# A decoder layer on one core: moments of two norms as ScalarE passes, and the feed-forward product behind the third block

## The chip, the cores and the metric

The kernel runs on one core of a Trainium2 chip. A core has five engines, each with its own queue of instructions that it works through in order: TensorE (PE in the profile, with its weight loads as PEld), VectorE (DVE), ScalarE (ACT), GpSimd (POOL) and SyncE (SP, which here issues the DMAs). They meet only at semaphores: an instruction that needs another engine's result waits, and everything behind it on its engine waits with it. The metric is the device time in microseconds, median of several runs.

## The reference

Three sublayers, each followed by a layer norm: causal attention, a long convolution, and a linear layer, the first and last with ternary weights and 8-bit activations. Cut to what the change touches:

```python
def _layernorm(x, axis=-1, eps=1e-05):
    m = jnp.mean(x, axis=axis, keepdims=True)
    v = jnp.var(x, axis=axis, keepdims=True)
    return (x - m) / jnp.sqrt(v + eps)

# convolution: x is (16 batches, 256 rows, 512), 32 heads of 8 rows, causal along the 512
kv = jnp.einsum('bhil,bhjl->bijhl', k_, v_)
y = irfft(rfft(kv, n=1024) * rfft(ssm_kernel, n=1024), n=1024)[..., :512]
out = jnp.einsum('bijhl,bhil->bjhl', y + kv * D, q_)

# linear layer on each row of 512
rms = rsqrt(mean(x * x) + 1e-06)
xn = x * rms * gamma
a_scale = 127.0 / (max(abs(xn)) + 1e-05)
x_q = clip(round(xn * a_scale), -128.0, 127.0) / a_scale
ffn = x_q @ w_q.T          # w_q ternary

x = _layernorm(x + attention(x))
x = _layernorm(x + convolution(ctx, ctx, x))
x = _layernorm(x + ffn(x))
```

The two norms of this case are the second and the third. The second norm's moments also give the root mean square that the linear layer divides by.

## The kernel before, in words

The attention comes first and takes about half of the time; the change doesn't touch it. It leaves the normed activations in `x1t`, turned so that the 512 positions lie along the partitions.

The second stage treats the 32 heads of the convolution one after another, with one repetition of a Python loop per head. A head has 8 rows in 16 batches, so its result is a tile of 128 x 512. The convolution is done as matrix products with a Toeplitz matrix of taps, `w`, cut into four blocks of 128 positions. Because it is causal, output block `lb` needs the input blocks 0 to `lb`: blocks 0, 1, 2 and 3 need 1, 2, 3 and 4 of them. Each is two products of 288 columns in float32, which the trace records as two matmuls each; so the four blocks show as x4, x8, x12 and x16 on L785.

For each head the engines do this:

- **GpSimd** multiplies the context with itself shifted (`multiply`, L754) into `kv`, and ScalarE squares it (`square`, L760). After each block GpSimd sums the parts (`add`, L960 and L962).
- **TensorE** makes the block's product `y` (`products`, L785) and turns the summed parts back into rows of 512 (`read`, L820), which gives `tok`. `y` has two accumulators, so a block takes the one that the block two before it has left: block 1 of a head can't start before VectorE has read block 3 of the head before.
- **VectorE** multiplies `y` with the queries in five instructions per block (`with_queries`, L797 to L812).
- **The second norm** of the previous head, `tok`, is made in the same repetition. `second_moments` takes mean and variance; `engine_roots` (L845, ScalarE), `newton` (L851 VectorE, L855 ScalarE) and `inverse_roots` (L863) make inverse roots out of a quarter of each variance; `second_centred` (L878) makes the centred, weighted row `xn`, `second_max` (L882) its largest size, and `second_norm` the normed row `x2` (L888), the scale, and the integers `fi` (L899 and L188).
- **The linear layer**: `turn` has the integers transposed by a DMA into `fit` (L904, on SP's queue); `feed_forward` multiplies them with the weights (L909), adds `x2` (L911, which gives `r3`) and takes the moments of `r3`; `finish` makes the third norm (L926) and sends it out (L927).

Both sets of moments come from VectorE: `bn_stats` (L835), `bn_aggr` (L837) and, for each root that is needed, the scaled variance `quarter` (L840). The square roots of `r3` of one head and of `tok` of the next are taken together, in one call with three columns.

The order on every engine is written out by hand: the stage runs inside `manual_schedule`, and each engine gets its instructions in the order in which the Python code issues them. So the place of a call in the loop sets its place in the queue of every engine that it uses. `on(stage, h, ...)` calls a stage for head `h` where there is such a head. In repetition `h` the blocks of head `h` are made, the second norm of head `h - 1`, and the linear layer and third norm of head `h - 2`. `last_heads` ends the work for the last two heads.

Of the kernel before, what the change touches and what calls it, by code (L numbers as in the profile page):

```python
# [9 lines left out]
F32 = mybir.dt.float32  # L10
# [5 lines left out]
P = 128  # L16
# [16 lines left out]
def decoder_kernel(ctx: ExitStack, tc: tile.TileContext, x, ctx_t, w_q, w_k, w_v, w_o, ker, d_skip, gamma, w_f, out):  # L33
# [695 lines left out]
    with ExitStack() as l2:  # L729
# [2 lines left out]
        ps_y = l2.enter_context(tc.tile_pool(name="ps_y", bufs=2, space=PSUM, side="right"))  # L732
        pb = l2.enter_context(tc.tile_pool(name="pb", bufs=1, side="right"))
        gam = pb.tile([P, E], F32, name="gam")
        op = l2.enter_context(tc.tile_pool(name="op", bufs=4, side="right"))


# [93 lines left out]
        FORMS = ((1.0, LN_EPS), (1.0, LN_EPS), (1.0 + RMS_EPS, RMS_EPS * LN_EPS))  # L831

        def moments2(src, roots, forms):
            st = sm.tile([P, 6], F32, name="st2")
            nc.vector.bn_stats(st, src)  # L835
            mv = sm.tile([P, 2], F32, name="mv2")
            nc.vector.bn_aggr(mv, st)  # L837
            for i in forms:
                a, b = FORMS[i]
                nc.vector.tensor_scalar(roots.quarter[:, i : i + 1], mv[:, 1:2], a / 4, b / 4, ALU.mult, ALU.add)  # L840
            return mv[:, 0:1]

        def engine_roots(roots):
            c = roots.cols
# [19 lines left out]

        def shifted(mean, res):
            shift = sm.tile([P, 1], F32, name="shift")
            nc.vector.tensor_scalar(shift, mean, res, -1.0, ALU.mult, ALU.mult)
            return shift

        def second_moments(m, roots):  # L870


            m.flat = m.tok.rearrange("p c k -> p (c k)")
            m.mean = moments2(m.flat, roots, (1, 2))

        def second_centred(m):
            m.xn = fp.tile([P, E], F32, name="xn")
            nc.vector.scalar_tensor_tensor(m.xn, m.flat, m.mean, gam, ALU.subtract, ALU.mult)  # L878

        def second_max(m):  # L880
            m.amax = sm.tile([P, 1], F32, name="amax2")
            nc.vector.tensor_reduce(m.amax, m.xn, AX.X, ALU.max, apply_absolute_value=True)  # L882

        def second_norm(m, roots, early_max=False):
            rstd, both = (roots.res[:, i : i + 1] for i in (1, 2))
            shift = shifted(m.mean, rstd)
            m.x2 = fp.tile([P, E], F32, name="x2")
            nc.scalar.activation(m.x2, m.flat, AF.Identity, bias=shift, scale=rstd)  # L888
            if not early_max:
                second_max(m)  # L890
            amax = m.amax
            nc.vector.tensor_scalar(amax, amax, both, 1e-5, ALU.mult, ALU.add)
            mul = sm.tile([P, 1], F32, name="mul2")
            nc.vector.reciprocal(mul, amax)
            nc.vector.tensor_scalar(mul, mul, both, 127.0, ALU.mult, ALU.mult)
            m.inv = sm.tile([P, 1], F32, name="inv2")
            nc.vector.tensor_scalar(m.inv, amax, w_inv[:, 4:5], 1.0 / 127.0, ALU.mult, ALU.mult)
            m.ft = fp.tile([P, E], F32, name="fq_t", tag="q_t")
            nc.scalar.activation(m.ft, m.xn, AF.Copy, bias=MAGIC, scale=mul)  # L899
            m.fi = rounded(fp, "fq", m.ft)  # L900

        def turn(m):
            m.fit = fp.tile([P, NB, P], BF16, name="fit")
            nc.sync.dma_start_transpose(m.fit, m.fi)  # L904

        def feed_forward(m, roots):
            acc = ps2.tile([P, E], F32, name="acc_f", tag="misc")
            for c in range(NB):
                nc.tensor.matmul(acc, m.fit[:, c, :], wf[:, c, :], start=(c == 0), stop=(c == NB - 1))  # L909
            m.r3 = fp.tile([P, E], F32, name="r3")  # L910
            nc.vector.scalar_tensor_tensor(m.r3, acc, m.inv, m.x2, ALU.mult, ALU.add)  # L911
            m.mean3 = moments2(m.r3, roots, (0,))

        def finish(m, roots, h, shared=False):
# [65 lines left out]
        def roots_of(cols):  # L980
            roots = Roots()
            roots.quarter = sm.tile([P, 3], F32, name="quarter")
            roots.root = sm.tile([P, 3], F32, name="root")
            roots.cols = cols
            return roots

        def last_heads():

            prev, last = heads[XH - 2 :]
            two, one, end = roots_of(slice(1, 3)), roots_of(slice(0, 1)), roots_of(slice(0, 1))  # L990
            read(last, 2)
            read_all(last, 3)
            second_moments(last, two)
            engine_roots(two)
            second_centred(last)
            newton(two)
            second_max(last)
            inverse_roots(two)
            second_norm(last, two, early_max=True)
            feed_forward(prev, one)  # L1000
            last.fit = fp.tile([P, NB, P], BF16, name="fit")
            transposed(ps2, last.fit, last.fi)
            engine_roots(one)
            newton(one)
            inverse_roots(one)
            finish(prev, one, XH - 2)
            feed_forward(last, end)
            engine_roots(end)
            newton(end)
            inverse_roots(end)  # L1010
            finish(last, end, XH - 1, shared=True)
# [5 lines left out]
        with tc.manual_schedule(engines=by_hand):  # L1017
            load(first_head, 0)
            load(heads[1], 1)
            nc.sync.dma_start(gam, gamma.partition_broadcast(P))  # L1020
            multiply(first_head, 1)
            multiply(first_head, 2)
            acc = {0: turn_sums(m, 0)}
            divide_sums(m)
            acc[1] = turn_sums(m, 1)
            keep(k, B - 3, (1,))
            m.ots, m.last = {}, {}
            for t in range(NT):
                divide(m, t, acc[t])
                out_scales(m, slice(t, t + 1))  # L1030
                m.ots[t] = scaled(ap, f"oq{t}", m.o[:, t, :], m.mul_o[t])
                if t == 0:
                    moments(n)
            multiply(first_head, 3)
            square(first_head)
            m.oit = kp.tile([P, NT, NB, P], BF16, name="oit")
            transposed(ps, m.oit[:, 0], rounded(ap, "oq0", m.ots[0]))
            close(m, slice(0, 1))
            transposed(ps, m.oit[:, 1], rounded(ap, "oq1", m.ots[1]))
            normalize(n)  # L1040
            moments_one(m, 0)
            keep(n, B - 2, (0,))
            multiplied(first_head, 0)
            normalize_one(m, 0)
            keep(m, B - 1, (0,))
            copy(first_head, slice(0, 1))
            copy(first_head, slice(1, NB))
            block(first_head, 0)
            close(m, slice(1, 2))
            moments_one(m, 1)  # L1050
            multiplied(first_head, 1)
            block(first_head, 1)
            normalize_one(m, 1)
            keep(n, B - 2, (1,))
            multiplied(first_head, 2)
            keep(m, B - 1, (1,))
            l1.close()
            fp = l2.enter_context(tc.tile_pool(name="fp", bufs=2))
            sm = l2.enter_context(tc.tile_pool(name="sm", bufs=3))
            ps_k = l2.enter_context(tc.tile_pool(name="ps_k", bufs=2, space=PSUM))  # L1060
            ps2 = l2.enter_context(tc.tile_pool(name="ps2", bufs=2, space=PSUM))


            for h in range(XH):
                roots = roots_of(slice(0 if h > 1 else 1, 3))

                on(load, h + 2, h + 2)
                on(add, h - 1, 3)
                on(block, h, 0)
                on(read, h - 1, 2)  # L1070
                on(multiply, h + 1, 1)
                on(square, h + 1)

                on(block, h, 1)
                on(feed_forward, h - 2, roots)
                on(add, h, 0)
                on(read, h - 1, 3)
                on(multiply, h + 1, 2)
                on(second_moments, h - 1, roots)
                if h > 0:  # L1080
                    engine_roots(roots)
                on(second_centred, h - 1)
                if h > 0:
                    newton(roots)

                on(block, h, 2)
                on(copy, h + 1)
                if h > 0:
                    inverse_roots(roots)
                on(add, h, 1)  # L1090
                on(read, h, 0)
                on(finish, h - 2, roots, h - 2)
                on(multiply, h + 1, 3)
                on(second_norm, h - 1, roots)

                on(block, h, 3)
                on(add, h, 2)
                on(read, h, 1)
                on(turn, h - 1)
            last_heads()  # L1100


# [35 lines left out]
```

## Time and profile before

| | us |
|---|---|
| median of 3 runs | 863.49 (861.42 to 866.24) |
| profiled execution | 861.06 |
| its span, first to last instruction | 859.2 |

The profiled execution lasts 1.9 us longer than its span. Its busy time by stage, in us:

| stage | length | PE | PEld | DVE | ACT | POOL | granted clock of TensorE |
|---|---|---|---|---|---|---|---|
| attention, 0 to 439.8 | 439.8 | 400.88 | 270.64 | 339.25 | 251.57 | 219.72 | 1.00 |
| handover, to 460.3 | 20.5 | 18.08 | 13.06 | 7.90 | 9.05 | 10.11 | 0.83 |
| head loop, to 842.9 | 382.6 | 371.84 | 271.48 | 335.67 | 159.39 | 352.67 | 1.00 |
| end, to 859.2 | 16.3 | 3.71 | 1.34 | 8.48 | 5.96 | 0.00 | 0.70 |

Times on the timeline count from the start of the span. A line gives start and length, engine, line of the code, operation, what it writes and reads, and in brackets how long the engine had been idle before it and what released it. Lengths of neighbours on one engine can overlap a little. In a line of waits the three numbers are the total, how many, and the longest.

### The profile page before, as it was taken

The page shows a single profiled execution, that of the slowest core. Times are in us where ns is not written, and L with a number is a line of the kernel's source. Part 1 is how long each engine was busy: PE and PEld are TensorE (multiplying, and loading weights), DVE is VectorE, ACT ScalarE, POOL GpSimd, SP SyncE. Part 2 cuts the span into 40 slices and gives each one's busy share as a digit, 9 for nine tenths or more (in the row PEclk, how much of TensorE's full clock was granted, in tenths as well). Part 3 has the DMA queues.
Part 4 walks back from the last instruction along what each step waited for, and adds up shares of the span by engine and source line. Part 5 has one row for each costly group of instructions (what it writes and reads, how often), then busy time and mean ns, then how long its engine had stood idle before and what let it go on. Part 6 is the DMA issues. An engine that isn't in the chain of part 4 may idle for free.

```text
span 859.2 us, 20181 instructions
## 1 busy us (share of the span) xinstructions
PE 794.5 (92%) x7677; PEld 556.5 (65%) x7754; DVE 691.3 (80%) x1889; ACT 426.0 (50%) x707; POOL 582.5 (68%) x652
## 2 busy tenths in 40 slices
PE   4889999999999999998878999999999999999993
PEld 3556666666666666665546777776777677777772
DVE  6757887788888778876665888988898888889886
ACT  6555655556565555655654334434443444344334
POOL 5265544545454454544638999999999999999980
PEclk9999999999999999999989999999999999999997
DMA  9121222233122222211320332333233323333311
GB/s 318 45 54 33 66 69 69 76 76 73 29 63 67 71 75 76 51 39 30 91 66 13 87 98 69 91 87 96 70 91 88 95 72 80 99 87 75 85 37 43
DMA packets 102207, 64.51 MB, mean 75 GB/s; under 512 B 66464, under 2 KB 83104, under 8 KB 102112
## 3 DMA queue, kind: packets, MB, share of 16 engines
q1 hardware_dynamic: 102112, 63.23, 27.5%
q8 instruction: 61, 1.00, 0.5%
q14 instruction: 34, 0.28, 0.1%
HBM read 43.34 MB, written 8.47 MB: 60 GB/s over the span
## 4 chain that ended last, share of the span: by engine, by line
PE 67%; DVE 12%; POOL 8%; ACT 6%; issue 6%; DMA 1%; ACTq 0%; DVEq 0%; POOLq 0%
PE y L785 23%; PE s L341 6%; PE acc L293 6%; PE s L381 5%; ACT p L386 4%; PE pv L409 4%; PE s L334 4%; DVE nmax L346 3%; PE acc_o L482 3%; POOL own L960 3%; PE acc_f L909 3%; POOL kv L754 3%; PE tok L820 3%; PE sums L416 2%; PE s L374 2%
## 5 line engine op out<-in xcount | busy, mean ns | idle before, releaser
L785 PE MATMUL y<-kv,w 128*128 128x288 f32 x1280 | 336.5, 410 | 3.7 <-DVE turn L812 2.7
L785 PEld LDWEIGHTS y<-kv,w 128*128 128x128 f32 x1280 | 234.7, 191 | 64.6 <-PE tok L820 8.5
L960 POOL TENSOR_TENSOR own<-own,turn 128x512 f32<-128x512 f32 x127 | 161.5, 1272 | 23.2 <-DVE turn L812 12.0
L390 POOL TENSOR_SCALAR_AFFINE_SELECT p<-p 128x512 f32<-128x512 f32 x128 | 81.0, 657 | 139.8 <-ACT p L386 129.5
L754 POOL TENSOR_TENSOR kv<-c 128x512 f32<-128x512 f32 (+1 forms) x128 | 144.0, 1136 | 2.9 <-PE sums L416 2.9
L346 DVE TENSOR_REDUCE nmax<-s 128x4 f32<-128x512 f32 (+1 forms) x128 | 116.5, 952 | 35.5 <-PE s L341 35.5
L386 ACT ACTIVATE p<-s 128x1536 f32<-128x1536 f32 x64 | 92.9, 1452 | 70.3 <-PE s L381 70.2
L845 ACT ACTIVATE root<-quarter 128x3 f32<-128x3 f32 (+2 forms) x34 | 6.9, 204 | 203.1 <-DVE quarter L840 203.0
L396 POOL TENSOR_TENSOR both<-p 128x512 f32<-128x512 f32 x64 | 82.3, 1285 | 5.3
L797 DVE SCALAR_TENSOR_TENSOR own<-y,q 128x128 f32<-128x128 f32 x128 | 36.0, 282 | 48.7 <-PE y L785 41.2
L962 POOL TENSOR_TENSOR own<-own 128x256 f32<-128x256 f32 x95 | 69.1, 727 | 7.5
L293 PE MATMUL acc<-xit,w 128*128 128x256 bf16 x504 | 68.9, 276 | 3.4 <-DVE w L158 3.2
L800 DVE TENSOR_TENSOR own<-y,q 128x384 f32<-128x384 f32 x128 | 70.0, 547 | 0.1
L803 DVE TENSOR_TENSOR turn<-y,q 128x384 f32<-128x384 f32 x128 | 70.0, 547 | 0.0
L293 PEld LDWEIGHTS <-w 128*128 128x128 bf16 x512 | 46.0, 99 | 24.0 <-issue 8.5
L820 PEld LDWEIGHTS tok<-ident,own 128*128 128x128 f32 x318 | 40.1, 141 | 32.7 <-POOL own L962 15.5
L820 PE MATMUL tok<-ident,own 128*128 128x128 f32 x318 | 57.2, 278 | 3.6 <-issue 1.2
L341 PE MATMUL s<-kt,qt 32*128 32x128 f32 (+1 forms) x1024 | 60.0, 348 | 0.0
L381 PE MATMUL s<-qt,kt 32*128 32x256 f32 (+1 forms) x1024 | 57.4, 335 | 0.0
L409 PE MATMUL pv<-p,va 128*32 128x256 f32 (+1 forms) x1024 | 54.9, 332 | 0.0
L421 ACT COPY ot<-pv 128x256 f32<-128x256 f32 x64 | 23.8, 373 | 50.9 <-PE pv L409 50.2
L334 PE MATMUL s<-mask,ident_h 128*128 128x256 bf16 x256 | 38.3, 271 | 11.1 <-ACT p L386 9.9
(148 smaller groups left out, 1342.0 us busy)
## 6 DMA issues: line engine op xcount, KB each, us to landing
xt<-in_x SPq DMA_DIRECT2D x16, 512.0 KB, 4.3
xr<-in_x SPq DMA_DIRECT2D x16, 512.0 KB, 4.7
c<-in_ctx_t SPq DMA_DIRECT2D x32, 256.0 KB, 3.3
w<-taps SPq DMA_DIRECT2D x32, 256.0 KB, 4.0
out_y<-res SPq DMA_DIRECT2D x31, 256.0 KB, 2.0
c<-in_ctx_t SPq DMA_DIRECT2D x32, 128.0 KB, 3.2
x1t<-in_w_q SPq DMA_DIRECT2D x1, 1024.0 KB, 6.4
x1t<-in_w_k SPq DMA_DIRECT2D x1, 1024.0 KB, 9.3
```

The source lines that it names most:

```text
L293: nc.tensor.matmul(acc[:, j, :], w[:, c, o * P : (o + 1) * P], m.xit[:, c].rearrange("p t k -> p (t k)"), start=(c == 0), stop=(c == NB - 1),)
L341: nc.tensor.matmul(s[:, r, lo:hi], m.qt[rows, g, q0 : q0 + P], m.kt[rows, g, 0:nk], start=False, stop=True, skip_group_check=True,)
L346: nc.vector.tensor_reduce(m.nmax[:, t, :, g], s[:, :, cols], AX.X, ALU.max, negate=True)
L381: nc.tensor.matmul(s[:, r, lo:hi], m.kt[rows, g, k0 : k0 + P], m.qt[rows, g, q0:S], start=False, stop=True, skip_group_check=True,)
L386: nc.scalar.activation(p, s[:, :, 0 : 3 * P], AF.Exp)
L390: nc.gpsimd.affine_select(out=own, in_=own, compare_op=ALU.is_ge, fill=0.0, base=0, pattern=[[0, 4], [1, P]], channel_multiplier=-1,)
L396: nc.gpsimd.tensor_tensor(both, p[:, :, P : 2 * P], p[:, :, 2 * P : 3 * P], ALU.add)
L409: nc.tensor.matmul(acc[rows, q0:S], m.va[:, j, 4 * g + r, :], p[:, r, src], start=(j == 0), stop=(j == 1), skip_group_check=True, tile_pos ...
L754: nc.gpsimd.tensor_tensor(kv[:, :, at : at + n * B].rearrange("p c (i b) -> p c i b", b=B), c[:, :, i : i + n, :], c[:, :, i + d : i + d + ...
L785: nc.tensor.matmul(y[:, Y0 + k * HALF : Y0 + (k + 1) * HALF], lhs, kv[:, mb, k * HALF : (k + 1) * HALF], start=(mb == 0), stop=(mb == lb),)
L820: nc.tensor.matmul(tok[:, lb, :], lhsT=own[:, d, :], rhs=ident, is_transpose=True, start=(d == last), stop=(d == 0))
L960: nc.gpsimd.tensor_tensor(own[:, 0:4, :], own[:, 0:4, :], turns[lb], ALU.add)
```

## The change

It does three things. The moments of both norms are no longer made by `bn_stats` and `bn_aggr` on VectorE, but by three ScalarE operations each: a copying pass whose accumulator gives the sum of the row, a step on one column that makes minus the mean, and a squaring pass with that as bias, whose accumulator gives the sum of squares. What the passes write is not used (`unused`). VectorE makes `quarter` out of the sum of squares.

The product of the linear layer is taken out of `feed_forward` (new: `feed_product`) and stands behind block 2, before it stood behind block 1. The rest of `feed_forward` stands between block 2 and block 3. Its roots are taken in the next repetition, together with the next head's, and `finish` comes one head later (`h - 3`). `last_heads` ends three heads instead of two.

Inside a repetition some calls are put in another order: `second_max` stands ahead of block 2, `second_norm` and `turn` ahead of `finish`, and the copies of the next head's queries behind that.

```diff
+        unused = pb.tile([P, E], BF16, name="unused")
...
         def moments2(src, roots, forms):
-            st = sm.tile([P, 6], F32, name="st2")
-            nc.vector.bn_stats(st, src)
-            mv = sm.tile([P, 2], F32, name="mv2")
-            nc.vector.bn_aggr(mv, st)
+            total = sm.tile([P, 1], F32, name="total2")
+            nc.scalar.activation(unused, src, AF.Copy, accum_out=total)
+            minus_mean = sm.tile([P, 1], F32, name="minus_mean")
+            nc.scalar.activation(minus_mean, total, AF.Copy, scale=-1.0 / E)
+            squares = sm.tile([P, 1], F32, name="squares")
+            nc.scalar.activation(unused, src, AF.Square, bias=minus_mean, accum_out=squares)
             for i in forms:
                 a, b = FORMS[i]
-                nc.vector.tensor_scalar(roots.quarter[:, i : i + 1], mv[:, 1:2], a / 4, b / 4, ALU.mult, ALU.add)
-            return mv[:, 0:1]
+                nc.vector.tensor_scalar(
+                    roots.quarter[:, i : i + 1], squares, a / (4 * E), b / 4, ALU.mult, ALU.add
+                )
+            return minus_mean
...
         def shifted(mean, res):
-            nc.vector.tensor_scalar(shift, mean, res, -1.0, ALU.mult, ALU.mult)
+            nc.vector.tensor_scalar(shift, mean, res, None, ALU.mult)
...
-            nc.vector.scalar_tensor_tensor(m.xn, m.flat, m.mean, gam, ALU.subtract, ALU.mult)
+            nc.vector.scalar_tensor_tensor(m.xn, m.flat, m.mean, gam, ALU.add, ALU.mult)
...
-        def second_norm(m, roots, early_max=False):
+        def second_norm(m, roots):
...
-            if not early_max:
-                second_max(m)
...
+        def feed_product(m):
+            m.acc = ps2.tile([P, E], F32, name="acc_f", tag="misc")
+            for c in range(NB):
+                nc.tensor.matmul(m.acc, m.fit[:, c, :], wf[:, c, :], start=(c == 0), stop=(c == NB - 1))
+
         def feed_forward(m, roots):
-            acc = ps2.tile([P, E], F32, name="acc_f", tag="misc")
-            for c in range(NB):
-                nc.tensor.matmul(acc, m.fit[:, c, :], wf[:, c, :], start=(c == 0), stop=(c == NB - 1))
             m.r3 = fp.tile([P, E], F32, name="r3")
-            nc.vector.scalar_tensor_tensor(m.r3, acc, m.inv, m.x2, ALU.mult, ALU.add)
+            nc.vector.scalar_tensor_tensor(m.r3, m.acc, m.inv, m.x2, ALU.mult, ALU.add)
             m.mean3 = moments2(m.r3, roots, (0,))
...
-        def last_heads():
+        def last_heads(three):
-            prev, last = heads[XH - 2 :]
-            two, one, end = roots_of(slice(1, 3)), roots_of(slice(0, 1)), roots_of(slice(0, 1))
+            early, prev, last = heads[XH - 3 :]
+            one, end = roots_of(slice(0, 1)), roots_of(slice(0, 1))
...
-            second_norm(last, two, early_max=True)
+            second_norm(last, three)
+            finish(early, three, XH - 3)
+            feed_product(prev)
             feed_forward(prev, one)
...
             finish(prev, one, XH - 2)
+            feed_product(last)
             feed_forward(last, end)
...
+            def roots_for(h):
+                return roots_of(slice(0 if h > 2 else 1, 3))
+
+            ahead = roots_for(0)
             for h in range(XH):
-                roots = roots_of(slice(0 if h > 1 else 1, 3))
+                roots, ahead = ahead, roots_for(h + 1)
...
                 on(block, h, 1)
-                on(feed_forward, h - 2, roots)
                 on(add, h, 0)
                 on(read, h - 1, 3)
...
+                on(second_max, h - 1)
 
                 on(block, h, 2)
-                on(copy, h + 1)
+                on(feed_product, h - 2)
                 if h > 0:
                     inverse_roots(roots)
                 on(add, h, 1)
                 on(read, h, 0)
-                on(finish, h - 2, roots, h - 2)
                 on(multiply, h + 1, 3)
                 on(second_norm, h - 1, roots)
+                on(turn, h - 1)
+                on(finish, h - 3, roots, h - 3)
+                on(copy, h + 1)
+                on(feed_forward, h - 2, ahead)
 
                 on(block, h, 3)
                 on(add, h, 2)
                 on(read, h, 1)
-                on(turn, h - 1)
-            last_heads()
+            last_heads(ahead)
```

More of the change, by code (lines that the diff above doesn't have):

```diff
@@ L985, in roots_of @@
             return roots
-        def last_heads():
-            prev, last = heads[XH - 2 :]
-            two, one, end = roots_of(slice(1, 3)), roots_of(slice(0, 1)), roots_of(slice(0, 1))
+        def last_heads(three):
+            early, prev, last = heads[XH - 3 :]
+            one, end = roots_of(slice(0, 1)), roots_of(slice(0, 1))
             read(last, 2)
             read_all(last, 3)
-            second_moments(last, two)
-            engine_roots(two)
+            second_moments(last, three)
+            engine_roots(three)
             second_centred(last)
-            newton(two)
+            newton(three)
             second_max(last)
-            inverse_roots(two)
-            second_norm(last, two, early_max=True)
+            inverse_roots(three)
+            second_norm(last, three)
+            finish(early, three, XH - 3)
+            feed_product(prev)
             feed_forward(prev, one)
```

## The prediction

> **What bounds the kernel now.** I read the engine shares and the chain that ended last first, then the waits inside two repetitions of the head loop, then its timeline.
>
> ```profile
> PE 794.5 (92%) x7677; PEld 556.5 (65%) x7754; DVE 691.3 (80%) x1889; ACT 426.0 (50%) x707; POOL 582.5 (68%) x652
> PE 67%; DVE 12%; POOL 8%; ACT 6%; issue 6%; DMA 1%; ACTq 0%; DVEq 0%; POOLq 0%
> ```
>
> TensorE is busy 92% of the span and two thirds of the last chain is its work. ScalarE is half idle, VectorE is not. The change touches only the last stage, one repetition per head. From the end of one block 3 on VectorE (L812 ends at 471.75) to the last (842.93) are 30 repetitions, so 371.18 / 30 = 12.37 us each. The waits from 586.5 to 611.2 us, two repetitions (total us, times, longest):
>
> ```profile
> DVE own L797 <- PE y L785: 2.1, 2, 1.0
> PEld tok L820 <- POOL own L962: 1.0, 2, 0.5
> PEld L909 <- DMA fit<-fq_i: 0.7, 2, 0.4
> ```
>
> TensorE loses little: 0.5 us for POOL's sums and 0.35 us for the transposed integers `fit`. VectorE waits for TensorE. So TensorE bounds the loop, and VectorE is close behind. One repetition on the timeline (start, length, engine, line):
>
> ```profile
> 595.70 0.21 DVE L812 TENSOR_TENSOR turn<-y,q 128x64 f32<-128x64 f32 x1
> 596.06 1.27 POOL L960 TENSOR_TENSOR own<-own,turn 128x512 f32<-128x512 f32 x1 [0.58 <-PE tok L820]
> 596.07 2.18 PE L785 MATMUL y<-kv,w 128*128 128x288 f32 x8
> 597.41 0.72 POOL L962 TENSOR_TENSOR own<-own 128x256 f32<-128x256 f32 x1
> ...
> 601.54 0.69 DVE L835 BATCH_NORM_STATS2 st<-tok 128x6 f32<-128x512 f32 x1
> ...
> 602.48 0.22 DVE L840 TENSOR_SCALAR quarter<-mv 128x1 f32<-128x1 f32 x2
> ...
> 602.61 0.74 DVE L878 SCALAR_TENSOR_TENSOR xn<-tok,mv,gam 128x512 f32<-128x512 f32 x1
> ...
> 603.35 0.26 DVE L797 SCALAR_TENSOR_TENSOR own<-y,q 128x128 f32<-128x128 f32 x1
> ...
> 604.92 0.34 DVE L867 TENSOR_SCALAR shift<-mv,res 128x1 f32<-128x1 f32 x2
> ...
> 605.17 0.81 ACT L926 ACTIVATE res<-r,shift,res 128x512 f32<-128x512 f32 x1
> ...
> 605.89 0.76 ACT L888 ACTIVATE x<-tok,shift,res 128x512 f32<-128x512 f32 x1
> ...
> 606.58 0.72 ACT L899 ACTIVATE fq_t<-xn,mul 128x512 f32<-128x512 f32 x1
> ...
> 606.77 0.29 DVE L797 SCALAR_TENSOR_TENSOR own<-y,q 128x128 f32<-128x128 f32 x1
> ...
> 607.33 0.63 ACT L188 ACTIVATE fq_i<-fq_t 128x512 bf16<-128x512 f32 x1
> ...
> 608.03 0.21 DVE L812 TENSOR_TENSOR turn<-y,q 128x64 f32<-128x64 f32 x1
> ```
>
> The reader is to see that block 3 on VectorE (L797 at 606.77 to L812) waits for no ScalarE result: it starts 0.1 us after TensorE's product, while ScalarE still works on the integers.
>
> **The change, part by part.** It takes two statistics, two aggregates from VectorE per head: 2 x (0.69 + 0.18) = 1.74 us. It gives ScalarE two times three operations. It moves the product behind block 2, one repetition after its `fit` was sent, so the 0.37 us wait goes (12.7 us over the loop). It moves the transposing DMA ahead of the output on SP's queue; its reader now comes a repetition later, so that costs nothing, as does the output DMA's own step (one head later, with the loop as cover). The single-operand `shift` keeps its 0.21 us row.
>
> What it adds is a wait. In the new order VectorE's queue holds, between block 2 and block 3: `r3`, then `quarter` from `squares` of that same `r3`, then block 3's five reads. `quarter` waits for ScalarE, and ScalarE's queue holds `x2`, `fq_t`, `fq_i`, the output, two copies of the queries ahead of the two passes. Behind block 3 wait POOL's sum, TensorE (block 1 of the next head takes block 3's accumulator) and the next head's block 0.
>
> Price of a moment on ScalarE. The nearest rows are the sums of weights at the start:
>
> ```profile
> 8.26 1.04 ACT L132 ACTIVATE w<-x1t 128x1024 bf16<-128x1024 f32 x1
> 9.20 0.19 ACT L132 ACTIVATION_READ_ACCUMULATOR w<-x1t 128x1 f32 x1
> ```
>
> 1024 columns take 0.94 us to the read and 0.19 for it. At 512 columns a plain pass takes 0.63 (L188), with the next 0.1 before its end, so 0.53 + 0.19 = 0.72; 0.70 out of the accumulator bank. A bias column adds 0.09 (L899 against L188): 0.80. The one-column step between takes 0.20 (like L845). With 0.03 at each handover a moment is 0.71 + 0.20 + 0.80 + 0.1 = 1.80, against 0.94 on VectorE (601.54 to 602.48). Bounds for each of the four passes: 0.54 (fq_i to the next start, no read paid) and 1.00 (L926's 0.81 plus the read). I take 0.71 and 0.80, since L132 is this very operation. The ends are -0.86 and +0.98 us per head, -26 and +29 us.
>
> Now the loop, from the end of block 3's reads (0; in the lines above 595.91):
> - POOL's two sums end at 598.13, so 2.22. TensorE's block 1 fills that time. Two transposes, 0.44 from 2.27: `tok` is whole at 2.71, ScalarE starts at 2.75.
> - Moments of `tok` 1.80: `quarter` at 4.55. VectorE has done blocks 0 and 1 by 3.9 and waits.
> - `quarter` to `xn` 0.13, `xn` 0.74, the maximum 0.69: block 2 at 6.11. L797 to `shift` 1.57: 7.68. From `shift` to `fq_t` 0.99, as at the end of the kernel (846.38 to 847.37): 8.67.
> - ScalarE: `fq_t` 0.75, `fq_i` 0.54, output 0.72, copies 0.51 and 0.34: 11.53. (`r3` has been done since 9.4.)
> - Moments of `r3` 1.84 out of SBUF: `quarter` at 13.37. Then 0.10, and block 3's reads 1.47: 14.94.
>
> So a repetition takes 14.9 us instead of 12.37. TensorE is no longer the bound: its block 3 is done at 10.5, the next block 0 and transposes at 12.5. What VectorE saved becomes waiting. 30 repetitions x 2.53 = 76; the first has no output (-0.7), the last no copies (-0.85): +74.3.
>
> The end: before, the last `fit` copy starts 6.30 us after block 3 (849.23), after it 9.22: moments of `tok` +0.85, a third column of roots +0.27, and ahead of the copy now stand an output and the moments of head 30 (+1.80). The last `r3` brings +0.87 more: +3.8. Without clock effects the sum is 861.06 + 74.3 + 3.8 = 939.
>
> **The clock.** TensorE will stand from 12.5 to 15.05, 2.55 us, in every repetition. Two stretches of before, one granted-clock window (3.41 us) long each, tell what that does (second column length, third TensorE busy):
>
> ```profile
> 449.90:453.31 3.41, 1.40 (x10) 1.14 (x11) 1.42 (x5) 3.41 (x6) 3.41 (x5) 1.00 0.00 0
> 842.51:845.92 3.41, 1.47 (x10) 0.79 (x9) 2.72 (x10) 0.81 (x4) 0.00 (x0) 1.00 0.19 38
> ```
>
> At the end of the first the granted clock went to 0.50 (453.4 to 456.8), at the end of the second it stayed at 1.00. So a window with under about 1.43 us of work, 1.98 idle, halves the next 3.41 us. Changes at 436.3, 443.15, 453.4, 456.8 and 849.3 lie on one grid of 3.41. A 2.55 us gap fills 1.98 of a grid window in (3.41 - 2.55 + 2 x 0.57) / 3.41 = 59% of positions. The slow stretch then begins between 0.57 before and 1.43 after block 1's start. At half clock a matmul takes 0.53 instead of 0.24 (four in 2.12 at 440.88), so block 1 and its transposes come 2.1 us later in 28% of these cases and 1.2 on average in the others: 1.4 mean. Estimate: 0.59 x 1.4 x 30 = 25, taken as 23 since a late block 1 also shortens the next gap a little. Bounds: 0, and 2.1 x 30 = 63.
>
> The Trainium skill ("TensorE: Matmul & The Clock Gate", "HAM oscillation") asks for no idle gap over about 3.4 us. By that rule the 2.55 us gaps are harmless and the sum is 939. The first stretch above holds no gap over 1.2 us and yet the clock fell, so I go by the row and 962.
>
> **The sum:** 861.06 (span 859.2 and 1.9 around it; 2.4 under the median of 863.49) + 74.3 + 3.8 + 23 = 962.
>
> **Rivals.**
> - The serial loop at full clock: 939. For it: a 2.55 us gap with dense work on both sides is seen nowhere in before. Against it: the 1.40 row.
> - A halved clock in every repetition: 939 + 63 = 1002. It needs the gap to hold the grid in step; 14.9 and 3.41 are not in step.
> - Faster: TensorE stays the bound, the moments vanish in ScalarE's idle half, and the `fit` wait goes: 861 - 12.7 = 848, with the 0.5 us before block 1 too 833. It decides as soon as the loop from block 3 to block 3 is under 12.37, that is, if 2.5 of my 14.9 us run beside the rest. For it: ScalarE's 50% and VectorE's lost 1.74 us. Against it: even at the low bound of the passes the loop is 14.1; and a queue holds block 3 behind `quarter`.
> - The wait stands elsewhere: if `quarter` of `r3` cost block 3 nothing, block 3 would follow TensorE at 10.5 + 1.6 and the loop would be 12.1 to 12.4: 861 + 3.8 for the end, less up to 8, so 857 to 865. Against it: the built order.
>
> **How the numbers follow.** Serial loop with partial clock drops 0.62, full clock 0.22, drops always 0.10, faster 0.04, nothing changed 0.02. Predicted is the first, 962. The range: down to 939 less half of the low bound of the passes (13), 926; up to 962 + 29 for the high bound, 991. That leaves out most of the always-halved case and both small ones. Measurements of this kernel tell 0.5% (about 4 us) from no change: faster 0.04, same 0.02, slower 0.94.
>
> **What would show it.** Right: VectorE idles about 4 us per head ahead of the single `quarter` from `squares`, released by ScalarE (some 120 us over the loop); TensorE's block 1 waits for VectorE's last read of block 3; ScalarE's 199 us of waiting at `root` shrink; the L132-like read of 0.19 follows each pass; the granted clock in the loop is about 0.9. Wrong: a repetition under 13 us, or block 3's reads starting right after TensorE's product. A loop near 14.9 at clock 1.00 speaks for the second case; one well over 16, for the third.

## The result, and the profile after

The changed kernel takes 955.33 us (median of 4 runs, 953.57 to 956.17) against 864.87 us for the kernel before in the same comparison: 1.105 times as long, with a 95% interval of 1.101 to 1.109. The prediction was 962 us.

The page of the profiled execution, engine shares and the chain that ended last:

```profile
span 952.8 us, 20390 instructions
PE 824.2 (87%) x7754; PEld 574.7 (60%) x7754; DVE 635.7 (67%) x1761; ACT 532.4 (56%) x1027; POOL 583.1 (61%) x652
...
PE 47%; ACT 24%; DVE 19%; issue 8%; POOL 1%; DMA 0%; ACTq 0%; DVEq 0%; POOLq 0%
```

VectorE has lost 56 us of work and ScalarE has gained 106, and in the head loop no engine is near full (TensorE 353.48 of the 420 us from 480 to 900). The chain tells it: TensorE's part fell from 67% to 47%, ScalarE's rose from 6% to 24%. A chain that passes through three engines in turn while all of them have idle time is a serial loop. The waits inside the head loop, 480 to 900 us (total, times, longest):

```profile
DVE quarter L844 <- ACT unused L841: 122.2, 54, 3.9
...
POOL own L966 <- DVE turn L813: 98.6, 27, 4.6
...
PE y L786 <- DVE turn L813: 66.5, 27, 2.7
...
DVE own L798 <- PE y L786: 35.3, 24, 2.7
```

VectorE waits for the squaring pass, and TensorE and GpSimd wait for VectorE's last read of a block (L813), 2.5 us and 3.7 us per head. Before, VectorE waited for TensorE, and TensorE and GpSimd hardly for VectorE (2.5 and 10.2 us over the whole loop). The 122.2 us at `quarter` are two waits per head, 3.88 us for `r3` and 0.66 us for `tok` in the lines below. One repetition at full clock, from one block 3 to the next (start, length, engine, line):

```profile
655.57 0.22 DVE L813 TENSOR_TENSOR turn<-y,q 128x64 f32<-128x64 f32 x1
...
655.93 2.18 PE L786 MATMUL y<-kv,w 128*128 128x288 f32 x8 [2.38 <-DVE turn L813]
...
658.59 0.60 ACT L837 ACTIVATE unused<-tok 128x512 bf16<-128x512 f32 x1 [3.89 <-PE tok L821]
...
660.36 0.22 DVE L844 TENSOR_SCALAR quarter<-squares 128x1 f32<-128x1 f32 x2 [0.66 <-ACT unused L841]
...
661.87 0.28 DVE L798 SCALAR_TENSOR_TENSOR own<-y,q 128x128 f32<-128x128 f32 x1
```

```profile
664.39 0.71 ACT L903 ACTIVATE fq_t<-xn,mul 128x512 f32<-128x512 f32 x1
664.40 0.74 DVE L917 SCALAR_TENSOR_TENSOR r<-acc_f,inv,x 128x512 f32<-128x512 f32 x1
...
667.18 0.63 ACT L837 ACTIVATE unused<-r 128x512 bf16<-128x512 f32 x1
...
668.17 0.72 ACT L841 ACTIVATE unused<-r,minus_mean 128x512 bf16<-128x512 f32 x1
668.80 0.19 ACT L841 ACTIVATION_READ_ACCUMULATOR unused<-r,minus_mean 128x1 f32 x1
...
669.02 0.15 DVE L844 TENSOR_SCALAR quarter<-squares 128x1 f32<-128x1 f32 x1 [3.88 <-ACT unused L841]
669.10 0.29 DVE L798 SCALAR_TENSOR_TENSOR own<-y,q 128x128 f32<-128x128 f32 x1
...
670.37 0.21 DVE L813 TENSOR_TENSOR turn<-y,q 128x64 f32<-128x64 f32 x1
```

`r3` is done at 665.14, and then VectorE stands for 3.88 us: `quarter` waits for ScalarE, which has four other things to do first, and block 3 (L798 at 669.10) stands behind `quarter`.

Where the 93.6 us between the spans went, by the ends of block 3 on VectorE: up to the one from which the prediction counts, nothing (471.68 against 471.75). The 30 repetitions take 461.05 instead of 371.18, that is +89.9. The end takes 20.07 instead of 16.27, +3.8. The repetitions come in two lengths: 14.80 us and, in 15 of the 30, about 16.0.

The longer ones are the clock (e6 below shows it). In the repetition before the one above, block 1 takes 3.26 us where it takes 2.18 above. First its line, then stretches of that repetition (columns: stretch, length, busy PE, PEld, DVE, ACT and POOL, granted clock, DMA share, GB/s):

```profile
639.97 3.26 PE L786 MATMUL y<-kv,w 128*128 128x288 f32 x8 [2.53 <-DVE turn L813]
```

```profile
638.00:639.00 1.00, 0.00 (x0) 0.00 (x0) 0.74 (x3) 0.74 (x3) 0.00 (x0) 1.00 0.55 139
...
640.50:641.00 0.50, 0.50 (x3) 0.38 (x2) 0.50 (x3) 0.00 (x0) 0.50 (x1) 0.91 0.65 160
641.00:642.00 1.00, 1.00 (x3) 0.67 (x2) 0.21 (x2) 0.00 (x0) 0.92 (x3) 0.50 0.30 90
...
644.00:645.00 1.00, 1.00 (x5) 0.79 (x4) 0.82 (x4) 0.94 (x4) 1.00 (x2) 0.84 0.00 0
```

TensorE stood from 637.4 to 640. At about 640.91 the granted clock fell to 0.50, and some 3.4 us later it was back. The 15 long repetitions are 18.4 us above 15 of 14.80. What is left of the 89.9, 71.5 us, is the serial loop at full clock.

### The profile page after: what moved, and what is told of

It is laid out like the page before. It is cut to its first block, busy times and chain, and to the rows that moved or that the text cites. A ratio compares the mean times of both kernels' runs of the same rounds, so it can differ in the third digit from the quotient of the medians.

```text
span 952.8 us, 20390 instructions
## 1 busy us (share of the span) xinstructions
PE 824.2 (87%) x7754; PEld 574.7 (60%) x7754; DVE 635.7 (67%) x1761; ACT 532.4 (56%) x1027; POOL 583.1 (61%) x652
## 4 chain that ended last, share of the span: by engine, by line
PE 47%; ACT 24%; DVE 19%; issue 8%; POOL 1%; DMA 0%; ACTq 0%; DVEq 0%; POOLq 0%
PE y L786 10%; PE s L341 6%; PE acc L293 5%; PE s L381 5%; ACT unused L837 4%; ACT p L386 4%; PE pv L409 3%; PE s L334 3%; ACT unused L841 3%; PE acc_o L482 3%; DVE own L801 3%; DVE turn L804 3%; DVE nmax L346 3%; ACT res L932 2%; ACT fq_t L903 2%
## 5 line engine op out<-in xcount | busy, mean ns | idle before, releaser
L786 PE MATMUL y<-kv,w 128*128 128x288 f32 x1280 | 359.5, 431 | 71.9 <-DVE turn L813 71.9
L786 PEld LDWEIGHTS y<-kv,w 128*128 128x128 f32 x1280 | 247.8, 202 | 138.6 <-issue 77.7
L844 DVE TENSOR_SCALAR quarter<-squares 128x1 f32<-128x1 f32 x96 | 11.8, 151 | 142.8 <-ACT unused L841 142.8
L837 ACT ACTIVATE unused<-tok 128x512 bf16<-128x512 f32 x32 | 19.1, 597 | 138.6 <-PE tok L821 136.3
L798 DVE SCALAR_TENSOR_TENSOR own<-y,q 128x128 f32<-128x128 f32 x128 | 36.8, 288 | 62.6 <-PE y L786 46.2
L821 PEld LDWEIGHTS tok<-ident,own 128*128 128x128 f32 x318 | 42.9, 149 | 33.7 <-POOL own L968 12.9
L821 PE MATMUL tok<-ident,own 128*128 128x128 f32 x318 | 60.6, 291 | 2.0 <-issue 1.2
```

Source lines behind the costliest of these rows:

```text
L786: nc.tensor.matmul(y[:, Y0 + k * HALF : Y0 + (k + 1) * HALF], lhs, kv[:, mb, k * HALF : (k + 1) * HALF], start=(mb == 0), stop=(mb == lb),)
L821: nc.tensor.matmul(tok[:, lb, :], lhsT=own[:, d, :], rhs=ident, is_transpose=True, start=(d == last), stop=(d == 0))
```

## The experiments

Three theories were set against each other. The one of the prediction: VectorE's queue holds block 3 behind `quarter` of `r3`, so everything ahead of `quarter` lies in series. Rival A: the passes cost their own length on ScalarE, wherever the wait stands. Rival B: the product's new place is what costs. All edits are against the changed kernel. Times are medians of 4 or 10 executions where they come with an interval (of the ratio to the kernel before), else of a single one.

**e1, the one-column `quarter` of `r3` later.** All passes and all orders stay; only one instruction of 0.15 us moves behind blocks 0 and 1 of the next head.

```diff
+            if late is not None:
+                late.squares = squares
+                return minus_mean
...
+        def feed_quarter(m, roots):
+            a, b = FORMS[0]
+            nc.vector.tensor_scalar(roots.quarter[:, 0:1], m.squares, a / (4 * E), b / 4, ALU.mult, ALU.add)
...
-            m.mean3 = moments2(m.r3, roots, (0,))
+            m.mean3 = moments2(m.r3, roots, (0,), late)
...
                 on(multiply, h + 1, 2)
+                on(feed_quarter, h - 3, roots)
                 on(second_moments, h - 1, roots)
```

> Only VectorE's one-column instruction that makes the quarter variance of r3 moves: behind blocks 0 and 1 of the next head, beside the one for tok. All ScalarE passes stay. Theory (block 3 is held in VectorE's queue by that instruction): block 3 follows TensorE's product at about 10.6 us after the last block 3, plus 1.5, so a repetition takes 12.1 to 12.4 us and the kernel about 858 us (853 to 868). Rival A (the passes cost their own length on ScalarE wherever the wait stands): no change, 950 to 957. Rival B (the product's new place is what costs): also 950 to 957.

Measured: 867.55 us, ratio 1.0039 (1.0018 to 1.006), repetitions of 12.40 us. Almost the whole loss is gone with one small instruction moved. What is left is the end of the kernel: from the last block 3 (845.91) to the end of the span (865.9) it takes 20.0 us, as in the changed kernel, against 16.27 before. Its timeline in the loop:

```profile
621.23 0.29 DVE L798 SCALAR_TENSOR_TENSOR own<-y,q 128x128 f32<-128x128 f32 x1 [1.56 <-PE y L786]
...
624.99 0.20 PEld L821 LDWEIGHTS tok<-ident,own 128*128 128x128 f32 x2 [0.41 <-POOL own L975]
...
626.55 0.14 DVE L920 TENSOR_SCALAR quarter<-squares 128x1 f32<-128x1 f32 x1
```

Block 3 on VectorE (621.23) waits for TensorE again, and the moved `quarter` (L920) waits for nobody. ScalarE does the same work as in the changed kernel, TensorE's product stands in the same place: rivals A and B fall.

**e2, the moments of `r3` back on VectorE; e3, those of `tok` back on VectorE.** Each takes one half of the passes from ScalarE. `moments_bn` is the code of before (`bn_stats`, `bn_aggr`, `quarter`); what reads the mean is put back with it.

```diff
 # e2
-            m.mean3 = moments2(m.r3, roots, (0,))
+            m.mean3 = moments_bn(m.r3, roots, (0,))
 # e3
-            m.mean = moments2(m.flat, roots, (1, 2))
+            m.mean = moments_bn(m.flat, roots, (1, 2))
```

> The moments of r3 go back to VectorE (statistics and aggregate), those of tok stay on ScalarE. Theory: the wait for ScalarE ahead of block 3 is replaced by about 0.95 us of VectorE's own work, done at 10.4 us, before TensorE's block 3; a repetition takes 12.1 to 12.4 us, the kernel about 857 us (852 to 868). Rival A (each ScalarE moment costs its own share): half of the loss comes back, about 908 us. Rival B: 950 to 957.

> The moments of tok go back to VectorE, those of r3 stay on ScalarE. Theory: nothing comes back. VectorE is busy with block 1 until 3.9 us, so its statistics give the quarter variances at 4.84 instead of 4.57 us; a repetition at full clock takes 15.0 to 15.1 instead of 14.8 us, and the kernel 950 to 970 us (the clock's part may shift). Rival A (each ScalarE moment costs its own share): half of the loss comes back, about 908 us.

Measured: e2 864.75 us, ratio 1.0012 (0.9995 to 1.003), repetitions of 12.39 to 12.40 (the first, as in e1 and before, 12.7). e3 970.05 us, repetitions of 15.04 at full clock and, in 20 of the 30, of 16.0 to 16.7. The two halves are not alike at all: one is worth everything, the other less than nothing. In e3 VectorE makes the statistics of `tok` as soon as it is free from block 1:

```profile
598.31 0.21 DVE L813 TENSOR_TENSOR turn<-y,q 128x64 f32<-128x64 f32 x1
...
602.22 0.21 DVE L813 TENSOR_TENSOR turn<-y,q 128x64 f32<-128x64 f32 x1
602.35 0.69 DVE L851 BATCH_NORM_STATS2 st<-tok 128x6 f32<-128x512 f32 x1
603.07 0.18 DVE L853 BATCH_NORM_AGGREGATE mv<-st 128x2 f32<-128x6 f32 x1
603.29 0.21 DVE L856 TENSOR_SCALAR quarter<-mv 128x1 f32<-128x1 f32 x2
```

Block 3 ends at 598.52, so `quarter` comes 4.77 us after it; in the changed kernel, where ScalarE works beside block 1, it is 4.57. This repetition takes 15.04 us, 0.24 more than 14.80, about what that step adds. Over 30 repetitions that is 7 of the 14.7 us that e3 is slower; the rest goes with the slowed repetitions, 20 instead of 15.

**e4, the query copies behind the passes of `r3`.** 0.85 us of ScalarE's queue leaves the series; the work is the same.

```diff
-                on(copy, h + 1)
                 on(feed_forward, h - 2, ahead)
+                on(copy, h + 1)
```

> The two copies of the next head's queries move from ahead of r3's two passes to behind them on ScalarE; nothing else. Theory (ScalarE's queue up to the squares of r3 lies in series): the loop shrinks by the copies' 0.51 + 0.34 = 0.85 us, to 13.95 us at full clock, so 26 us less over 30 repetitions: about 929 us, and down to 915 if the shorter gap also slows the clock less often. Rivals A and B (ScalarE's load, the product's place): the same work in the same repetition, 950 to 957.

Measured: 916.86 us. Repetitions take 13.96 us at full clock, 0.84 less, and only 4 of the 30 (15.14 us) are slowed by the clock, instead of 15. `quarter` still waits, 0.83 us less:

```profile
653.91 0.15 DVE L844 TENSOR_SCALAR quarter<-squares 128x1 f32<-128x1 f32 x1 [3.05 <-ACT unused L841]
```

So the 0.85 us taken out of ScalarE's queue ahead of `quarter` came back nearly in full. Of the 38 us, 25 are this (30 x 0.84), the rest is the clock. That a reordering of ScalarE alone is worth as much excludes rival A a second time.

**e5, the order alone.** Both moments on VectorE (e2 and e3 together); what is left is the product behind block 2 and the output one head later.

> Both sets of moments on VectorE as before; what is left of the change is the order: the product behind block 2, r3 and its statistics between blocks 2 and 3, the output one head later. Theory: no wait for ScalarE ahead of block 3, but VectorE's chain from block 3 to block 3 has both statistics in it: about 12.5 us a repetition by the rows, 865 us (858 to 873). Rival B (the product's place costs): well over 900 us. Rival C (the order alone would have been a gain by the 0.37 us wait that goes): 850 us.

Measured: 864.37 us, ratio 0.999 (0.9973 to 1.0007), repetitions of 12.39 to 12.40. The new order costs nothing and gains nothing, though the wait for `fit` is gone from it.

**e6, the gap filled.** Ten more products on TensorE ahead of block 1, into the accumulator that the product behind block 2 then overwrites.

```diff
+        def filler(m):
+            m.acc = ps2.tile([P, E], F32, name="acc_f", tag="misc")
+            for k in range(10):
+                c = k % NB
+                nc.tensor.matmul(m.acc, m.fit[:, c, :], wf[:, c, :], start=True, stop=True)
...
         def feed_product(m):
-            m.acc = ps2.tile([P, E], F32, name="acc_f", tag="misc")
+            if not hasattr(m, "acc"):
+                m.acc = ps2.tile([P, E], F32, name="acc_f", tag="misc")
...
                 on(read, h - 1, 2)
...
+                on(filler, h - 2)
                 on(block, h, 1)
```

> The changed kernel with ten more products of 128 columns of weights by 512 (2.2 us) on TensorE in the gap ahead of block 1; their values are overwritten by the product behind block 2. Theory (every second gap halves the clock, which costs 1.17 us): the granted clock stays at 1.00, all repetitions take 14.8 us, and the kernel gets about 17 us faster for more work: 938 us (933 to 945). Rival (the 16.0 us repetitions have another cause, such as DMA or queue phases): they stay, 953 to 960 us.

Measured: 942.83 us. TensorE is busy 49 us more in the stretch from 486 to 880 us, and the kernel is 12.5 us faster (changed kernel first, then e6):

```profile
486.00:880.00 394.00, 331.61 (x1379) 240.84 (x1380) 233.96 (x869) 215.74 (x534) 295.83 (x283) 0.94 0.26 68
```

```profile
486.00:880.00 394.00, 380.61 (x1681) 257.88 (x1707) 241.55 (x902) 226.64 (x558) 303.99 (x291) 1.00 0.27 72
```

The granted clock went from 0.94 to 1.00 and the repetitions in the steady part to 14.78 to 14.80 each. So the 16.0 us repetitions were the clock. Two things are missing to the 938. The first repetition with a filler lasts 3.1 us longer (17.42 against 14.32): there is no gap in it yet, and the added products wait 0.98 us for integers and take 2.1 themselves. And the part ahead of the loop, which the edit doesn't touch, ended 3.1 us later in this execution (474.74 against 471.68).

**e7, the product into the gap.** As e1, with the product ahead of block 1 and the copies ahead of the output.

```diff
+                on(feed_product, h - 2)
                 on(block, h, 1)
...
                 on(block, h, 2)
-                on(feed_product, h - 2)
...
-                on(finish, h - 3, roots, h - 3)
                 on(copy, h + 1)
+                on(finish, h - 3, roots, h - 3)
```

> The later quarter of e1, and in addition the product ahead of block 1, where TensorE waits for block 3's accumulator, and the query copies ahead of the output on ScalarE. Theory: TensorE's chain from block 1 to the end of block 3 on VectorE loses the product's 0.65 us: a repetition takes 11.4 to 11.9 us, the kernel 835 to 852 us, 844 likeliest. Rival (ScalarE's two moments then arrive too late for the next head, 11.5 + 1.84 us against the next tok at 2.75): a repetition at 12.3 or more, 862 us or more.

Measured: 885.36 us, ratio 1.0244 (1.0205 to 1.0283), repetitions of 12.98 us. A miss: the time is in the rival's range, but not by the rival's mechanism. TensorE in one repetition:

```profile
643.32 0.81 PE L916 MATMUL acc_f<-w,fit 128*128 128x512 bf16 x3 [1.40 <-DMA fit<-fq_i]
```

The integers of head h - 2 are sent near the end of repetition h - 1. Behind block 2 they are long there; ahead of block 1 they land 1.4 us too late. I had filled a wait with a new one.

**e8 and e9, the product of head h - 3 into the gap.** One head more between sending and product, ahead of the transposes that wait for GpSimd, with three buffers instead of two (five instead of three for the small columns); the `r3` moments of the last three heads on VectorE. e8 keeps e1's later `quarter`; e9 has the moments of `r3` on VectorE.

```diff
                 on(block, h, 0)
+                on(feed_product, h - 3)
                 on(read, h - 1, 2)
...
                 on(block, h, 2)
-                on(feed_product, h - 2)
...
-                on(finish, h - 3, roots, h - 3)
                 on(copy, h + 1)
-                on(feed_forward, h - 2, ahead)
+                on(finish, h - 4, roots, h - 4)
+                if h > 2:
+                    feed_forward(heads[h - 3], ahead, heads[h - 3])
```

This is e8, which also has e1's lines with `feed_quarter` one head later (`h - 4`). The last lines are `on(feed_forward_bn, h - 3, ahead)` in e9, where `feed_forward_bn` takes the moments with `moments_bn`.

> As e7 (later quarter, copies ahead of the output), but the product in the gap is that of one head earlier (h - 3, whose integers were sent a whole repetition before), and it stands ahead of the transposes that wait for GpSimd; the end of the kernel takes its last moments on VectorE. Theory: e7's 12.98 us came from waiting 1.4 us for integers just sent; without it TensorE's chain is 12.40 - 0.86 = 11.54 us, and GpSimd's 11 operations of a head (4 x 1.27 + 3 x 0.73 + 4 of L755, 4.5 together, 11.8 in all) become the bound: 11.9 us a repetition, the kernel about 850 us (844 to 857). Rival (something else in e7's order costs, such as the copies' place): 12.4 us or more, 862 us or more.

> The product of head h - 3 in the gap as in e8, but the moments of r3 stay on VectorE and only those of tok are ScalarE passes; no later quarter. Theory: block 3 waits on VectorE until about 10.3 us, TensorE's block 3 ends at 10.1, so 11.9 us a repetition, as GpSimd's bound: about 850 us (844 to 858). Rival (VectorE's r3 and statistics hold block 3): 12.2 or more, 858 us or more.

Measured: e8 846.39 us, ratio 0.9798 (0.9775 to 0.982), repetitions of 11.73; e9 851.44 us, ratio 0.9851 (0.9829 to 0.9872), repetitions of 11.85. Both are faster than the kernel before, by 2.0% and 1.5%, and so than the changed one. The head loop of e8, 484 to 812.5 us:

```profile
484.00:812.50 328.50, 327.04 (x1485) 246.71 (x1511) 254.32 (x951) 235.29 (x580) 321.84 (x309) 1.00 0.33 87
```

TensorE is busy 327.04 of 328.5 us, so it is TensorE that bounds e8 and not GpSimd (321.84), on which I had counted: the times of e8 and e9 came out within the stated ranges, with the bound misjudged. Here the ScalarE passes over `r3` pay: e8 is 5 us faster than e9, which has the moments of `r3` on VectorE; 4.1 us in the profiled executions are the 30 repetitions (352.2 against 356.3). No run has the product in the gap with both sets of moments on VectorE. So most of the gain over the kernel before may be the product's new place alone; how much the passes over `tok` add to it is open.

## Why the prediction was right

The direction, the mechanism and nearly every term of the sum held. Steps of the loop, in us from the end of block 3 (here 655.79); the last three rows are totals over the kernel:

| step | predicted | measured |
|---|---|---|
| ScalarE starts on `tok` | 2.75 | 2.80 |
| `quarter` of `tok` | 4.55 | 4.57 |
| block 2 on VectorE | 6.11 | 6.08 |
| `fq_t` | 8.67 | 8.60 |
| first pass over `r3` | 11.53 | 11.39 |
| `quarter` of `r3` | 13.37 | 13.23 |
| next block 3 read | 14.94 | 14.79 |
| 30 repetitions at full clock, more than before | 74.3 | 71.5 |
| the clock | 23 | 18.4 |
| end of the kernel, more than before | 3.8 | 3.80 |

**The price of a moment.** The weight sums at the kernel's start (L132) were the right row. The groups of the loop (busy us, mean ns):

```profile
L841 ACT ACTIVATE unused<-r,minus_mean 128x512 bf16<-128x512 f32 x29 | 20.9, 721 | 0.9
...
L837 ACT ACTIVATE unused<-r 128x512 bf16<-128x512 f32 x29 | 18.1, 625 | 0.0
...
L837 ACT ACTIVATION_READ_ACCUMULATOR unused<-r 128x1 f32 x29 | 5.4, 187 | 0.0
```

A moment of `r3` lasts from 667.18 to 668.99, 1.81 us (predicted 1.84).

**The clock.** The mechanism was right and the size a little off. 59% of the repetitions were to lose 1.4 us each; 15 of 30 lost 1.2 (18.4 us in all, 23 predicted). That it came so close is in part luck, for two steps of the estimate don't hold. The first is the 1.43 us of work below which a window was to halve the clock. The clock changed at 453.39, so the stretch that I had ended at 453.31 lay 0.08 us too early. Put in its place it holds 1.48 us, more than the 1.47 of the stretch after which the clock stayed; and of two stretches of e4 with the same 1.69 us of work, one was followed by the full clock and one by the halved (first before, then e4, each stretch with the one behind it):

```profile
449.98:453.39 3.41, 1.48 (x10) 1.22 (x11) 1.33 (x5) 3.41 (x6) 3.41 (x5) 1.00 0.00 0
```

```profile
525.51:528.92 3.41, 1.69 (x8) 1.22 (x9) 2.95 (x11) 1.70 (x5) 1.28 (x1) 1.00 0.69 203
528.92:532.33 3.41, 3.41 (x16) 2.48 (x15) 1.78 (x8) 1.72 (x6) 3.38 (x4) 1.00 0.26 66
539.17:542.58 3.41, 1.69 (x8) 1.07 (x7) 2.72 (x10) 2.00 (x5) 1.20 (x2) 1.00 0.85 204
542.58:545.99 3.41, 3.41 (x10) 2.36 (x9) 1.35 (x5) 0.69 (x2) 3.33 (x4) 0.50 0.46 74
```

So the busy time of a window, as the profile gives it, does not alone decide, and no run here shows a sharp limit. The second step is that the gaps would fall evenly on all positions of the grid; the last section shows that they didn't.

The rule of the Trainium skill ("TensorE: Matmul & The Clock Gate", "HAM oscillation"), no idle gap over about 3.4 us, taken as the limit would have given 939. Here gaps of 2.5 us were followed by a halved clock in every second repetition, and e6 shows that the clock stays when they are filled.

**The `fit` wait.** I counted its 0.37 us as gone and lost in the new wait. e5 shows that it would not have been a gain in any case. Before, TensorE's weight loads waited for `fit` behind block 1, and the transposes behind the product waited for nobody:

```profile
598.16 0.55 PEld L909 LDWEIGHTS <-fit 128*128 128x128 bf16 x4 [0.37 <-DMA fit<-fq_i]
...
598.83 0.36 PEld L820 LDWEIGHTS tok<-ident,own 128*128 128x128 f32 x2
```

In e1 (the line at 624.99 above) and e5 the same transposes, of block 3, stand directly behind block 1 and wait 0.41 us for GpSimd's sum. The product had covered that wait. In e5 there are two such waits per repetition (22.1 us in 54 between 484 and 812 us), before there was one (12.5 us in 26). So the rival that gave 848 us rested on a saving that wasn't there.

**The rivals.** Full clock (939) was excluded by the clock in the loop (0.94), always halved (1002) by every second repetition at 14.80, the two fast cases by the 122 us of waits at `quarter`. The case "nothing changed" gave 857 to 865 for a kernel where `quarter` costs block 3 nothing. e1 is that kernel, 3.9 us above the kernel before: its repetitions take 12.40, the upper end of the 12.1 to 12.4 that I had worked out. The lower end came from TensorE's block 3 ending at 10.5 us; in e1 VectorE starts to read it 10.9 us after the last one (621.23 against 610.32). Part of this is the product's own length, 0.86 us with four matmuls (661.25 to 662.11 in the changed kernel), where I had used 0.65 from three records.

## What to carry to other kernels

Work moved to a half-idle engine was free here only where the consumer's place in its own queue moved too: look at what is queued behind the first instruction that reads the moved result, and add up the idle engine's queue ahead of it. Before a one-column instruction that waits on another engine, put the work that doesn't need it. A gap on TensorE can be filled by a product whose inputs were sent a whole repetition earlier (e8 against e7), and a gap that stays can cost a second time through the clock (e6).

## What was not expected

The clock and the loop fell into step. The granted clock fell within each of these stretches of the changed kernel, at about 610.19, 640.91 and 671.63 us:

```profile
610.10:610.20 0.10, 0.10 (x2) 0.10 (x1) 0.10 (x2) 0.00 (x0) 0.10 (x1) 0.96 0.48 184
640.90:641.00 0.10, 0.10 (x2) 0.06 (x1) 0.10 (x3) 0.00 (x0) 0.10 (x1) 0.56 1.80 225
671.60:671.70 0.10, 0.10 (x2) 0.10 (x1) 0.10 (x2) 0.00 (x0) 0.10 (x1) 0.67 1.06 225
```

They are 30.72 us apart, nine steps of the 3.41 us grid, and two repetitions, 14.80 + 15.97 = 30.77 us, are nearly as long. So every second gap was caught. Over the loop the pair drifts by some 0.05 us each time; the long ones grow from 16.0 to 16.32, then two long ones follow each other and the pattern starts again. In e4 the gap is shorter (1.73 us at 640.48), and twice six repetitions of 13.96 and one of 15.14 (98.9 us, 29 steps) make the pattern. The prediction had the loop and the grid out of step, and took that against the case of a halved clock in every repetition. A slowdown by the clock can so look like a regular property of the loop.
